# Step sizes of a selective scan: one Softplus on ScalarE out of PSUM, in place of Abs, Relu, Exp, Ln and three GpSimd passes

## The chip, the core and the metric

One NeuronCore of a Trainium2 chip runs the whole kernel. The metric is the device time of one execution in microseconds (us), the median of several runs. Engine names in the profile: PE is TensorE, PEld its weight loads, DVE is VectorE, ACT is ScalarE, POOL is GpSimd, SP is SyncE, which here only issues DMAs. L795 means line 795 of the kernel before.

## What is computed

The reference has two layers on an image of 256 x 256 tokens with 128 channels: layer 0 is a normalised attention along rows (triangle attention), layer 1 a two-dimensional selective scan (the heart of a Mamba block). The change lies in layer 1, in its first line:

```python
def selective_scan(xs, dts, As, Bs, Cs, Ds, dt_bias):
    delta = jax.nn.softplus(dts + dt_bias[None, :, :, None])
    ...
    def step(h, inp):
        d_t, x_t, B_t, C_t = inp
        dA = jnp.exp(d_t[..., None] * As)
        h = dA * h + (d_t * x_t)[..., None] * B_t[:, :, None, :]
        y = jnp.einsum('bkdn,bkn->bkd', h, C_t)
        return (h, y)
```

There are four scan directions (K = 4), 65,536 tokens in each, 256 channels and 16 states per channel; everything is float32. `delta` is the step size: softplus(v) = ln(1 + exp(v)) of a projection v plus a bias for each channel.

## The kernel before, in words

Layer 0 and the convolution in front of the scan take the first 5.5 ms of the 32.2 ms. The scan takes the rest, and the change is in it.

**Steps, groups, turns.** The scan goes through the four directions one after another, in four passes of 128 steps; `steps` (L692) lists them. A step is 512 tokens of one direction. It has 8 groups of 32 channels (`g` from 0 to 7); a group's 32 channels by 4 states fill the 128 partitions, and the 16 states are four such sets. So a group has four turns (the loop `for n, i in enumerate((NB, *range(NB)))` in the last block of the kernel), and in each turn ACT makes one factor `dA` (exp(delta A), L1122) and DVE makes one `tensor_tensor_scan` over 512 tokens (L1148). In turn 0 ACT writes the factor `dAl` to SBUF (2 buffers) and the scan's other input, `bl`, comes from PE out of PSUM. In turns 1 to 3 the factor `dA` goes to PSUM (3 buffers) and the other input has been written by a DVE multiplication, `times_B` (L875, 128 x 1536), which DVE does once per group after turn 1. After a group's last scan POOL copies the last column (`hst`, L1167) and multiplies the group's states with C (L1168); PE sums these products (`sums`, L890) later.

**Who sets the order.** The scan is written under a manual schedule: each engine executes its instructions in the order in which the Python code issues them. The preparation of coming steps is therefore written as generators, and in each turn the main loop takes one piece of `prepare(q + 2)` (`piece(preparing)`), one of `turn`, one of each `finish` or `store`, and a given number of pieces of `products`. A `yield` is the end of a piece. All of this is issued in the turn after that turn's `dA` on ACT and before its scan on DVE.

**What `prepare(q)` does (L721 to L804).** It starts in turn 1 of group 5, two steps ahead of its use. PE turns the tokens (`tps`), ACT copies them (`xs`), PE projects them (`pb`), ACT copies that (`bc`, L747), and a DMA sends its B and C rows to DRAM (`bc_d`). PE then makes `pv`, the projected step size, for the two halves of the channels (L758, two PSUM banks out of a pool of two, tag `mm`). From there on, in the kernel before:

- first group of the next step, turns 1 and 2: for each half ACT computes `e` = |v| (Abs, L765) and `delta` = max(v, 0) (Relu, L766) from PSUM;
- turn 3: PE turns B (`tpb`, L770, in the bank pool that `pv` used), ACT computes `e` = exp(-e) (L773), SP issues the DMAs of `B_r` and `C_r` (L779);
- second group: ACT computes `lg` = 1 + e (L785), `du` = lg - 1 (L788) and copies `B_t` (L790); POOL computes e - du (L792), a correction for the rounding of 1 + e;
- third group: turn 0, ACT computes ln(lg) (L795), for which ACT loads another function table, and loads the table of Exp again for the next `dA` (L1122); turns 1 and 2, POOL adds twice (L797, L799) to get `delta`, and SP sends it to DRAM (`de_d`, L801); turn 3, POOL multiplies `du` = delta * xs (L803).

`spread_delta` (L851) brings `de_d` back into `dr`, spread over partitions, for the factors: the first half in group 5 of the step before its use, the second half at the start of group 1 of the step itself. `du` goes to PE for `spread_du` (L861) and `turn` (L806). In the fourth pass `finish` (L947) follows each step: normalisation, gate and output projection, with ACT operations `yn` (L989), `gz` (L1008), `xo` (L1032) and POOL operations of its own, spread over the following step and a half.

Of the kernel before, what the change touches and what calls it, by code (L numbers as in the profile page):

```python
# [8 lines left out]
F32 = mybir.dt.float32  # L9
BF16 = mybir.dt.bfloat16  # L10
AF = mybir.ActivationFunctionType
ALU = mybir.AluOpType
# [4 lines left out]
P = 128  # L17
# [6 lines left out]
DI = 256  # L24
NS = 16
R = 8
K = 4
T = 512
# [38 lines left out]
def attention_and_scan_kernel(  # L67
# [27 lines left out]
    nc = tc.nc  # L95
# [26 lines left out]
    with tc.tile_pool(name="gx", bufs=3) as gx, tc.tile_pool(  # L122
        name="gps", bufs=1, space=PSUM
# [41 lines left out]
    with tc.tile_pool(name="ln", bufs=3) as ln, tc.tile_pool(  # L165
        name="lnps", bufs=3, space=PSUM
# [100 lines left out]
    with tc.tile_pool(name="abias", bufs=1) as ab:  # L267

        bias = ab.tile([P, 2, H, S], F32, name="bias")
# [24 lines left out]
        with tc.tile_pool(name="ablk", bufs=2) as blk, tc.tile_pool(  # L294
            name="arow", bufs=2
        ) as row, tc.tile_pool(name="aps", bufs=2, space=PSUM) as aps:
            for b in range(S // RB):
# [18 lines left out]
                for q in range(BT // 512):  # L316
# [23 lines left out]
                    for rr in range(2):  # L340
# [5 lines left out]
                        for h in range(H):  # L346
# [14 lines left out]
                            for t in range(2):  # L361
# [4 lines left out]
                                    bias=mx[:, h, t : t + 1],  # L366
# [10 lines left out]
                        for h in range(H):  # L377
                            hp = (h % 2) * C
                            tp = aps.tile([P, 2, S], F32, name="atp")
# [57 lines left out]
    with tc.tile_pool(name="cw", bufs=1) as cw, tc.tile_pool(name="cs", bufs=2) as cs:  # L437
# [23 lines left out]
        with tc.tile_pool(name="g2", bufs=1) as g2, tc.tile_pool(  # L461
            name="g2ps", bufs=1, space=PSUM
        ) as g2ps:
            m2, r2 = group_norm_finish(nc, g2, g2ps, stats2, S // RB, ones, neg_half)
            for col, src in ((m_col, m2), (r_col, r2)):
                tp = g2ps.tile([P, P], F32, name="g2t", tag="g2t")
# [171 lines left out]
    sw = ctx.enter_context(tc.tile_pool(name="sw", bufs=1))  # L638
# [4 lines left out]
    dtb_s = sw.tile([P, K, 2], F32, name="dtb_s")  # L643
# [31 lines left out]
    for q in range(4):  # L675
# [1 line left out]
            spread[:, q],  # L677
            ident[:, 32 * q : 32 * q + 32].unsqueeze(1).to_broadcast([P, 4, 32]),
        )
    neg_one = sw.tile([P, 1], F32, name="neg_one")  # L680
    nc.vector.memset(neg_one, -1.0)
    hst = sw.tile([P, NG, NI], F32, name="hst")

    io = ctx.enter_context(tc.tile_pool(name="io", bufs=2))
    wk = ctx.enter_context(tc.tile_pool(name="wk", bufs=2))
    sd = ctx.enter_context(tc.tile_pool(name="sd", bufs=2, space=DRAM))
# [29 lines left out]
    def until(now, then):  # L716

        for _ in range(then - now):
            yield

    def prepare(q):  # L721

        k, a = steps[q]
        xt = loaded.pop(q)
        xs = io.tile([P, 2, T], F32, name="xs", bufs=3)
        tps = []
        for h in range(2):
            tp = sps.tile([P, T], F32, name="tps", tag="mm")
            for j in range(4):
                nc.tensor.transpose(  # L730
                    tp[:, j * P : (j + 1) * P], xt[:, j, h * P : (h + 1) * P], ident
                )
            tps.append(tp)
            yield
        yield from until(2, 5)
        for h, tp in enumerate(tps):
            nc.scalar.copy(xs[:, h, ::-1] if k >= 2 else xs[:, h, :], tp)
            yield
        pb = sps.tile([R + 2 * NS, T], F32, name="pb", tag="mm")
        for h in range(2):  # L740
            nc.tensor.matmul(  # L741
                pb, xw_in[:, k, h, :], xs[:, h, :], start=(h == 0), stop=(h == 1)
            )
        yield
        yield
        bc = io.tile([R + 2 * NS, T], F32, name="bc", bufs=1)
        nc.scalar.copy(bc, pb)  # L747
        bc_d = sd.tile([2 * NS, T], F32, name="bc_d")
        nc.sync.dma_start(bc_d, bc[R:, :])
        yield  # L750


        e = io.tile([P, 2, T], F32, name="e", bufs=1)
        delta = io.tile([P, 2, T], F32, name="delta", bufs=1)
        pvs = []
        for h in range(2):
            pv = sps.tile([P, T], F32, name="pv", tag="mm")
            nc.tensor.matmul(  # L758
                pv, dtw_s[:, k, h * P : (h + 1) * P], bc[:R, :], start=True, stop=True
            )  # L760
            pvs.append(pv)
        yield
        yield
        for h, pv in enumerate(pvs):
            nc.scalar.activation(e[:, h, :], pv, AF.Abs, bias=dtb_s[:, k, h : h + 1])  # L765
            nc.scalar.activation(delta[:, h, :], pv, AF.Relu, bias=dtb_s[:, k, h : h + 1])  # L766
            yield
        tp = sps.tile([P, 4, R + 2 * NS], F32, name="tpb", tag="mm")
        for b in range(4):
            nc.tensor.transpose(  # L770
                tp[:, b, :], bc[:, b * P : (b + 1) * P], ident[: R + 2 * NS, : R + 2 * NS]
            )
        nc.scalar.activation(e, e, AF.Exp, scale=-1.0)  # L773
        B_r = io.tile([P, NB, T], F32, name="B_r")
        C_r = io.tile([P, NI, T], F32, name="C_r")
        for m, t, ni in ((0, B_r, NB), (1, C_r, NI)):
            for j in range(4):
                n = m * NS + NI * j
                nc.sync.dma_start(  # L779
                    t[32 * j : 32 * j + 32],  # L780
                    bc_d[n : n + ni, :].unsqueeze(0).to_broadcast([32, ni, T]),
                )
        yield
        lg = io.tile([P, 2, T], F32, name="lg", bufs=1)
        nc.scalar.activation(lg, e, AF.Identity, bias=1.0)  # L785
        yield
        du = io.tile([P, 2, T], F32, name="du")
        nc.scalar.activation(du, lg, AF.Identity, bias=neg_one)  # L788
        B_t = io.tile([P, 4, R + 2 * NS], F32, name="B_t")
        nc.scalar.copy(B_t, tp)  # L790
        yield
        nc.gpsimd.tensor_tensor(e, e, du, ALU.subtract)  # L792
        yield
        yield
        nc.scalar.activation(lg, lg, AF.Ln)  # L795
        yield
        nc.gpsimd.tensor_tensor(lg, lg, e, ALU.add)  # L797
        yield
        nc.gpsimd.tensor_tensor(delta, delta, lg, ALU.add)  # L799
        de_d = sd.tile([DI, T], F32, name="de_d")  # L800
        nc.sync.dma_start(de_d.rearrange("(h p) t -> p h t", p=P), delta)  # L801
        yield
        nc.gpsimd.tensor_tensor(du, delta, xs, ALU.mult)  # L803
        prepared[q] = xs, de_d, du, B_r, C_r, B_t  # L804

    def turn(q):  # L806
# [272 lines left out]
    ctx.enter_context(tc.manual_schedule())  # L1079
    load(0)  # L1080
    preparing.append(prepare(0))
    drain(preparing)
    load(1)
# [5 lines left out]
    bxs[0, 0] = times_B(0, spread_du(0, 0))  # L1089
    urs[0, 1] = spread_du(0, 1)  # L1090
    preparing.append(prepare(1))
    for _ in range(2 * NI + 3):
        piece(preparing)
# [9 lines left out]
    for s, (q, g) in enumerate(all_steps):  # L1103
        k, a = steps[q]
# [12 lines left out]
        for n, i in enumerate((NB, *range(NB))):  # L1117
# [23 lines left out]
            if g == 5 and n == 1 and q + 2 < NQ:  # L1141
                preparing.append(prepare(q + 2))
# [91 lines left out]
```

## Time and profile before

| | |
|---|---|
| median of 3 runs | 32186.01 us (32183.83 to 32190.26) |
| the profiled execution, span from first to last instruction | 32185.1 us |
| mean granted TensorE clock | 0.853 |
| busy in the span | PE 23853.4, DVE 29575.2, ACT 25201.0, POOL 25710.4 us |
| first `times_B` of the four passes | at 5576, 12139, 18690 and 25241 us |
| end of the last scan | at 32134 us |

The profile is of one execution. Times in the timeline are us from the start of the span; a group's line gives its count, its busy time and the mean duration of one instruction, and then how long the engine was idle before such instructions, and which engine's work ended most of that idle time. Consecutive instructions of one engine overlap a little, so the distance from start to start (the pitch) is shorter than the duration. The span and the median differ by 1 us, so a sum made against the span can be read against the median.

### The profile page before, as it was taken

Reading aid. Unit: us, or ns where it says so; the run is one execution under the profiler, and the core shown is the slowest. Engines: PE = TensorE matmul, PEld = TensorE weight load, DVE = VectorE, ACT = ScalarE, POOL = GpSimd, SP = SyncE. Lnnn points to the kernel's source line nnn. Section 1 sums busy time; section 2 is a strip of 40 time slices with the busy share of each in tenths; the row PEclk is TensorE's granted clock in tenths of the full one; section 3 lists DMA queues with packets and bytes.
Section 4 is the critical chain, followed back from the end, with each engine's and each line's share of the span. In section 5 each row is a group of like instructions: output and inputs, shape, how many; then the busy total and the mean of one; then the engine's idle time right before and its main releaser. Section 6 shows DMA issues by size and latency. Waiting matters only on the chain.

```text
span 32185.1 us, 380702 instructions
## 1 busy us (share of the span) xinstructions
PE 23853.4 (74%) x122902; PEld 10868.3 (34%) x122902; DVE 29575.2 (92%) x29023; ACT 25201.0 (78%) x50438; POOL 25710.4 (80%) x11291
## 2 busy tenths in 40 slices
PE   6999988666676667777777777777777777777777
PEld 3555544222222222222222232223222333333333
DVE  7666633999999999999999999999999999999999
ACT  5555522888888888888888888888888888888888
POOL 4222200999999999999999999999999999999998
PEclk9999999888888888888888888888888888888888
DMA  4001033444444444444444444444444555555554
GB/s 143 30 28 29 27 105 121 110 109 108 111 109 108 110 110 118 119 121 120 119 120 122 119 119 121 121 119 119 122 119 118 123 124 124 123 123 123 124 123 113
DMA packets 2100469, 3518.55 MB, mean 109 GB/s; under 512 B 201112, under 2 KB 1187096, under 8 KB 2022560
## 3 DMA queue, kind: packets, MB, share of 16 engines
q1 hardware_dynamic: 2093296, 3476.09, 43.3%
q8 instruction: 967, 15.84, 0.2%
q10 hardware_dynamic: 5168, 18.12, 0.1%
q14 instruction: 1038, 8.50, 0.1%
HBM read 2754.18 MB, written 739.25 MB: 109 GB/s over the span
## 4 chain that ended last, share of the span: by engine, by line
PE 32%; ACT 24%; DVE 22%; issue 12%; POOL 9%; DMA 2%; SPq 0%; ACTq 0%; POOLq 0%; DVEq 0%
DVE bx L1148 11%; PE yp L890 8%; DVE bx L875 7%; ACT dA L1122 6%; PE ur L864 6%; POOL bx L1168 5%; PE pb L741 3%; ACT bt L834 2%; PE pc L563 2%; ACT dAl L1122 2%; PE av L393 2%; PE tpy L913 2%; POOL at L370 2%; ACT e L765 2%; ACT L795 2%
## 5 line engine op out<-in xcount | busy, mean ns | idle before, releaser
L1168 POOL TENSOR_TENSOR bx<-bx,C_r 128x2048 f32<-128x2048 f32 x4096 | 18604.4, 4542 | 334.3 <-POOL hst L1167 5.8
L1148 DVE TENSOR_TENSOR_SCAN bx<-dA,hst,bx 128x512 f32<-128x512 f32 x12192 | 15074.4, 1264 | 217.2 <-ACT dA L1122 215.3
L1122 ACT ACTIVATE dA<-dr,A_s 128x512 f32<-128x512 f32 x12288 | 8329.3, 683 | 2247.5 <-DVE bx L1148 2199.6
L864 PE MATMUL ur<-du,spread 128*128 128x512 f32 x8192 | 5710.1, 787 | 4498.5 <-DVE bx L875 4378.8
L875 DVE TENSOR_TENSOR bx<-B_r,ur 128x1536 f32<-128x1536 f32 x4096 | 7075.5, 1727 | 40.1 <-DMA dr<-de_d 40.1
L834 ACT ACTIVATE bt<-duT,B_t 128x128 f32<-128x128 f32 x16384 | 5572.5, 392 | 698.7 <-PE bl L846 698.7
L1148 DVE TENSOR_TENSOR_SCAN bx<-dAl,hst,bl 128x512 f32<-128x512 f32 x4064 | 5096.6, 1254 | 24.2 <-PE bl L846 24.1
L890 PE MATMUL yp<-bx,gather 128*32 128x512 f32 x32768 | 5052.5, 771 | 7.5 <-POOL bx L1168 6.4
L846 PE MATMUL bl<-ident,bt 128*128 128x128 f32 x16384 | 2714.8, 289 | 2441.0 <-DVE bx L1148 2439.0
L846 PEld LDWEIGHTS bl<-ident,bt 128*128 128x128 f32 x16384 | 1791.0, 143 | 4323.4 <-DVE bx L1148 3240.7
L864 PEld LDWEIGHTS ur<-du,spread 128*128 128x128 f32 x8192 | 1451.2, 223 | 5027.9 <-DVE bx L875 5023.9
L370 POOL TENSOR_TENSOR at<-at,sm 128x2048 f32<-128x2048 f32 x256 | 922.2, 3603 | 2719.7 <-DVE sm L369 2550.6
L1122 ACT ACTIVATE dAl<-dr,A_s 128x512 f32<-128x512 f32 x4096 | 2919.2, 713 | 0.0
L890 PEld LDWEIGHTS yp<-bx,gather 128*32 128x32 f32 x32768 | 1165.1, 139 | 4348.3 <-issue 3834.9
L1167 POOL COPY hst<-bx 128x4 f32<-128x4 f32 x4096 | 771.4, 188 | 1615.5 <-DVE bx L1148 1588.6
L362 ACT ACTIVATE at<-at,mx 128x256 f32<-128x256 f32 x2048 | 1016.1, 498 | 472.5 <-DVE mx L358 468.1
L792 POOL TENSOR_TENSOR e<-e,du 128x1024 f32<-128x1024 f32 x512 | 1202.8, 2349 | 138.3 <-DMA C_r<-bc_d 138.3
L799 POOL TENSOR_TENSOR delta<-delta,lg 128x1024 f32<-128x1024 f32 x512 | 1209.9, 2363 | 40.1
L803 POOL TENSOR_TENSOR du<-delta,xs 128x1024 f32<-128x1024 f32 x512 | 1205.4, 2354 | 40.2
L758 PE MATMUL pv<-bc,dtw_s 8*128 8x512 f32 x2048 | 1019.6, 616 | 256.5 <-ACT bc L747 256.5
L797 POOL TENSOR_TENSOR lg<-lg,e 128x1024 f32<-128x1024 f32 x512 | 1205.0, 2354 | 0.2 <-ACT lg L795 0.2
L391 DVE COPY aT<-atp 128x512 f32<-128x512 f32 x512 | 353.6, 691 | 774.8 <-PE atp L382 771.0
(173 smaller groups left out, 31933.7 us busy)
## 6 DMA issues: line engine op xcount, KB each, us to landing
dr<-de_d SPq DMA_DIRECT2D x4096, 256.0 KB
C_r<-bc_d SPq DMA_DIRECT2D x2048, 256.0 KB
B_r<-bc_d SPq DMA_DIRECT2D x2048, 192.0 KB
de_d<-delta SPq DMA_DIRECT2D x512, 512.0 KB
xtok<-xc_d SPq DMA_DIRECT2D x256, 512.0 KB
xtok<-xc_d SPq DMA_DIRECT2D x512, 256.0 KB
yl<-y_d SPq DMA_DIRECT2D x512, 256.0 KB
y_d<-yt SPq DMA_DIRECT2D x512, 256.0 KB
```

The source lines that it names most:

```text
L370: nc.gpsimd.tensor_tensor(at, at, sm.unsqueeze(3).to_broadcast([P, H, 2, S]), ALU.mult,)
L797: nc.gpsimd.tensor_tensor(lg, lg, e, ALU.add)
L799: nc.gpsimd.tensor_tensor(delta, delta, lg, ALU.add)
L803: nc.gpsimd.tensor_tensor(du, delta, xs, ALU.mult)
L834: nc.scalar.mul(bt[:, b, :, j, :], duT[:, b, h * P : (h + 1) * P].rearrange("t (g c) -> t g c", c=32), B_t[:, b, n : n + 1],)
L846: nc.tensor.transpose(bl[:, b * P : (b + 1) * P], bt[:, b, g % 4].rearrange("t j c -> t (j c)"), ident)
L864: nc.tensor.matmul(ur, spread[:, g % 4].rearrange("p j c -> p (j c)"), prepared[q][2][:, g // 4, :], start=True, stop=True,)
L875: nc.vector.tensor_tensor(bx[:, :NB, :], prepared[q][3], ur.unsqueeze(1).to_broadcast([P, NB, T]), ALU.mult,)
L890: nc.tensor.matmul(yp[32 * g : 32 * g + 32, :], gather, hc[:, i, :], start=(i == 0 and steps[q][0] != ORDER[0]), stop=True, skip_group_che ...
L1122: nc.scalar.activation(dA, dr, AF.Exp, scale=A_s[:, k, g // 4, g % 4, i : i + 1])
L1148: nc.vector.tensor_tensor_scan(hs[:, i, :], dA, hs[:, i, :] if i < NB else bls.pop((q, g)), 0.0 if a == 0 else hst[:, g, i : i + 1], ALU.mult,
L1168: nc.gpsimd.tensor_tensor(hs, hs, prepared[q][4], ALU.mult)
```

## The change

The softplus becomes one ACT instruction for each half, straight from `pv` in PSUM with the bias as operand. The buffers `e`, `lg` and the constant `neg_one` go. The DMA of `delta`, the multiplication `du`, the PE transposes of B, the copy `B_t` and the DMAs of `B_r` and `C_r` stay, in other places:

```diff
-    neg_one = sw.tile([P, 1], F32, name="neg_one")
-    nc.vector.memset(neg_one, -1.0)
...
-        e = io.tile([P, 2, T], F32, name="e", bufs=1)
         delta = io.tile([P, 2, T], F32, name="delta", bufs=1)
...
         for h, pv in enumerate(pvs):
-            nc.scalar.activation(e[:, h, :], pv, AF.Abs, bias=dtb_s[:, k, h : h + 1])
-            nc.scalar.activation(delta[:, h, :], pv, AF.Relu, bias=dtb_s[:, k, h : h + 1])
-            yield
+            nc.scalar.activation(
+                delta[:, h, :], pv, AF.Softplus, bias=dtb_s[:, k, h : h + 1]
+            )
+        de_d = sd.tile([DI, T], F32, name="de_d")
+        nc.sync.dma_start(de_d.rearrange("(h p) t -> p h t", p=P), delta)
+        yield
         tp = sps.tile([P, 4, R + 2 * NS], F32, name="tpb", tag="mm")
         for b in range(4):
             nc.tensor.transpose(
                 tp[:, b, :], bc[:, b * P : (b + 1) * P], ident[: R + 2 * NS, : R + 2 * NS]
             )
-        nc.scalar.activation(e, e, AF.Exp, scale=-1.0)
+        yield
+        du = io.tile([P, 2, T], F32, name="du")
+        nc.gpsimd.tensor_tensor(du, delta, xs, ALU.mult)
+        B_t = io.tile([P, 4, R + 2 * NS], F32, name="B_t")
+        nc.scalar.copy(B_t, tp)
+        yield
         B_r = io.tile([P, NB, T], F32, name="B_r")
         C_r = io.tile([P, NI, T], F32, name="C_r")
...
-        yield
-        lg = io.tile([P, 2, T], F32, name="lg", bufs=1)
-        nc.scalar.activation(lg, e, AF.Identity, bias=1.0)
-        yield
-        du = io.tile([P, 2, T], F32, name="du")
-        nc.scalar.activation(du, lg, AF.Identity, bias=neg_one)
-        B_t = io.tile([P, 4, R + 2 * NS], F32, name="B_t")
-        nc.scalar.copy(B_t, tp)
-        yield
-        nc.gpsimd.tensor_tensor(e, e, du, ALU.subtract)
-        yield
-        yield
-        nc.scalar.activation(lg, lg, AF.Ln)
-        yield
-        nc.gpsimd.tensor_tensor(lg, lg, e, ALU.add)
-        yield
-        nc.gpsimd.tensor_tensor(delta, delta, lg, ALU.add)
-        de_d = sd.tile([DI, T], F32, name="de_d")
-        nc.sync.dma_start(de_d.rearrange("(h p) t -> p h t", p=P), delta)
-        yield
-        nc.gpsimd.tensor_tensor(du, delta, xs, ALU.mult)
         prepared[q] = xs, de_d, du, B_r, C_r, B_t
```

In the order of instructions that ACT gets, a table load stands before the two Softplus and another before the next `dA`; the program has as many table loads as before, but for one in the very first step. They stand in turn 1 of the first group of a step instead of turn 0 of the third. The DMA of `de_d` stands in turn 1 of the first group (it was turn 2 of the third), the PE transposes `tpb` in turn 2 (was 3), `du` and `B_t` in turn 3 of the first group (were turn 3 of the third and turn 1 of the second), the DMAs of `B_r` and `C_r` in turn 0 of the second group (were turn 3 of the first). On SP the second half of `dr` now goes ahead of them.

## The prediction

> **What bounds the kernel now.** I read the page first, for the busy shares and their course over time:
>
> ```profile
> PE 23853.4 (74%) x122902; PEld 10868.3 (34%) x122902; DVE 29575.2 (92%) x29023; ACT 25201.0 (78%) x50438; POOL 25710.4 (80%) x11291
> ...
> DVE  7666633999999999999999999999999999999999
> ACT  5555522888888888888888888888888888888888
> POOL 4222200999999999999999999999999999999998
> ```
>
> DVE and POOL both show 9 in the scan (from slice 8 on), so shares do not say which of them sets the pace. The busy time in the four passes of the scan does (columns: stretch, its length, then PE, PEld, DVE, ACT, POOL):
>
> ```profile
> 5576.00:12139.00 6563.00, 4574.31 (x19427) 1793.22 (x19426) 6522.89 (x5118) 5554.67 (x10766) 5992.81 (x2558) 0.83 0.45 109
> 12139.00:18690.00 6551.00, 4663.03 (x20471) 1923.14 (x20470) 6524.59 (x5121) 5556.56 (x10753) 6000.74 (x2561) 0.83 0.49 120
> 18690.00:25241.00 6551.00, 4670.14 (x20481) 1930.03 (x20482) 6524.16 (x5121) 5557.31 (x10756) 6000.26 (x2561) 0.83 0.49 120
> 25241.00:32134.00 6893.00, 5056.47 (x23700) 2427.97 (x23698) 6730.30 (x6139) 5981.81 (x11599) 6495.85 (x3191) 0.82 0.51 123
> ```
>
> DVE is idle for 26 us of the second pass, and for 163 us of the fourth. It is the bound, and the change touches no DVE instruction. POOL's own waits are mostly for DVE (L1167: 1615.5 us idle, 1588.6 of it for the scan). So the large removals (three POOL passes of 2.35 us, 7.1 us per step) do not count by themselves; only DVE's waits do. Those of the fourth pass:
>
> ```profile
> DVE bx L1148 <- ACT dA L1122: 148.6, 125, 1.9
> ```
>
> 125 waits in 128 steps: one per step, at one place. The other passes have 27.4, 21.1 and 20.2 us of the same kind. The timeline of a step in the second pass shows the place, the Ln of the third group:
>
> ```profile
> 15016.30 0.73 ACT L1122 ACTIVATE dAl<-dr,A_s 128x512 f32<-128x512 f32 x1
> 15017.05 1.28 ACT L795 ACT_TABLE_LOAD   x1
> 15018.34 1.06 ACT L795 ACTIVATE lg<-lg 128x1024 f32<-128x1024 f32 x1
> ...
> 15019.42 1.28 ACT L1122 ACT_TABLE_LOAD   x1
> 15019.98 1.25 DVE L1148 TENSOR_TENSOR_SCAN bx<-dAl,hst,bl 128x512 f32<-128x512 f32 x1
> ...
> 15020.71 1.91 ACT L1122 ACTIVATE dA<-dr,A_s 128x512 f32<-128x512 f32 x3
> ...
> 15021.44 1.28 DVE L1148 TENSOR_TENSOR_SCAN bx<-dA,hst,bx 128x512 f32<-128x512 f32 x1 [0.20 <-ACT dA L1122]
> ```
>
> From 15017.05 to 15020.71 ACT makes no factor; the scan in turn 1 starts when the factor after it is there.
>
> **What the waits cost.** A group without waits takes 6.36 us (`times_B` starts at 15041.72 and next at 15048.08), eight take 50.88. The second pass took 6551/128 = 51.18 per step, so 0.30 us is lost: some 0.2 is shown as idle, the rest is overlap of instructions that a wait breaks. In three passes that is 384 x 0.30 = 115 us. In the fourth pass `finish` adds DVE work: there `times_B` at 28015.69 is followed by a scan at 28018.93, 3.24 us instead of 1.64, so a step without waits takes 50.88 + 1.57 = 52.45 (the scan behind it is 0.03 shorter). It took 6893/128 = 53.85: 1.40 lost, 179 us in the pass.
>
> **What is removed.** Per step ACT loses two Abs and two Relu from PSUM (0.57 us of pitch each), Exp, 1 + e and Ln (1.06 each) and `du` (1.15), and gets two Softplus. The Ln block leaves the third group, and with it the waits on L1122. The two table switches do not go; they move.
>
> **What is added, and its room.** In the first group, turn 1, ACT now does: load, Softplus, Softplus, load, and only then the next `dA`. A load is 1.283 us wherever it occurs (L795, L1122, and for other functions L313, L362). Softplus is in no row. Nearest is Abs of L765: the same PSUM tile, shape and bias operand, 0.673 us, pitch 0.57. The plain copy out of PSUM (L737, 0.577) bounds it from below, as an instruction of this shape; `gz` with two pointer operands (0.768) is the dearest single pass. I take Abs. As Softplus has to do what Abs, Relu, Exp and Ln did together, two passes (1.24 us) are the upper end, kept for a rival. The block then is 1.28 + 0.57 + 0.67 + 1.28, the next `dA` 0.68, and about 0.1 for gaps and the signal to DVE: 4.58 us. The rows of the turn before:
>
> ```profile
> 15005.45 0.67 ACT L1122 ACTIVATE dA<-dr,A_s 128x512 f32<-128x512 f32 x1
> 15006.07 0.67 ACT L765 ACTIVATE e<-pv,dtb_s 128x512 f32<-128x512 f32 x1
> ...
> 15011.25 2.45 DVE L1148 TENSOR_TENSOR_SCAN bx<-dA,hst,bx 128x512 f32<-128x512 f32 x2
> ```
>
> `dA` ends at 15006.12 and the next scan out of PSUM is due at 15011.25: room 5.13, margin 0.55. Abs started at 15006.07 without idle, so `pv` is ready. The block is hidden by two scans and `times_B`; without that cover it would cost all of 3.8 us. In these passes I cost it at nothing.
>
> In the fourth pass two `yn` (0.5 us of pitch each) stand ahead, and `bc` waits for PE:
>
> ```profile
> 28039.04 0.67 ACT L1122 ACTIVATE dA<-dr,A_s 128x512 f32<-128x512 f32 x1
> ...
> 28044.35 2.44 DVE L1148 TENSOR_TENSOR_SCAN bx<-dA,hst,bx 128x512 f32<-128x512 f32 x2
> ```
>
> Room 4.64 here. Over neighbouring steps it runs through 5.52, 4.64, 4.21, 3.99, 4.23 and again, as `yp` on PE takes between 4.1 and 5.8 us under the clock it is granted. Against 4.58 that misses by 0.37, 0.59 and 0.35 in three steps of five: 0.26 us on average, 0.31 with broken overlap, 40 us in the pass. The scan after it is due 1.2 us later and its factor takes 0.6, so it does not wait again.
>
> Waits for `bl` from PE (14 us in the fourth pass, 10 in the second and third) may shrink, since ACT is ahead in group 3, where `bl` depends on its products; I take it that these 24 us stay.
>
> **What is moved.** On POOL `du` comes before the first group's `hst`: POOL is free of the last product at 15012.2, ends `du` at 14.6 and starts `hst` 0.8 us late (it was 15013.76, after 1.5 idle); with the passes of the next groups gone it has caught up a group later. On SP the DMA of `de_d` now waits for Softplus (until about 15008.7) ahead of `dr`, `B_r`, `C_r`. That half of `dr` is needed three groups later, `B_r` and `C_r` a step later, and `C_r` waited for POOL until 15012.24 anyway. On PE `tpb` needs the bank of the first Softplus half, at 15008.0 instead of 15007.36; behind it `bl` waits for a scan until 15008.56. All hidden.
>
> **The start.** The very first step has nothing beside it: `pv` is done at 5555.4, `de_d` issued at 5569.9, first `times_B` at 5576.23. Now two Softplus end at 5556.7 (the load fits in ACT's wait of 1.2 us for `pv`); then SP issues `B_r` and `C_r`, 3.5 us, so `dr` goes out about 5561 instead of 5572.96: 12 us earlier, and the rest follows from it. If `B_r` lands late, 8.
>
> **Sum.** (115 - 10) + (179 - 40 - 14) + 12 = 242; 32185 - 242 = **31,943 us**, -0.75%.
>
> In the timeline above a load begins 0.02 us after the instruction before it and the next begins 0.01 us after the load: no drain on either side. The Trainium skill ("ScalarE: Activation LUTs", section "What ACT_TABLE_LOAD costs") speaks against this place: it gives a switch of sets 1283 ns and a drain of about 1380 ns, 2.66 us in all. By the page the block would be an estimated 7.3 us, 2.2 over the room in every step of three passes, and the change slower by some 900 us. The sum goes by the rows.
>
> **Rivals.**
>
> 1. *The wait moves with the block, and is dearer: slower.* The place is turn 1 of the first group; the mechanism is a Softplus longer than Abs. With x us more per step, three passes lose 384 (x - 0.47) once the margin is gone, the fourth 128 x. Together they reach 242 at x = 0.82, or 0.41 us per Softplus. Two passes each (1.24 us, x = 1.14) give 257 + 146 = 403: 31,943 + 403 = **32,346**. For it: no row has the function. Against: the instruction order shows one instruction per half, and Abs (0.673), Exp (0.683) and Sigmoid (0.688, L313) take alike for 512 elements. 10%.
> 2. *No change*: the same with x between 0.70 and 0.97, or unseen gaps of that size around the loads, 32,120 to 32,260. 6%.
> 3. *The fourth pass keeps its loss*, as the block meets `yn` and a late `bc` in every step: 32,185 - 105 - 12 = **32,068**. For it: the margin is negative in three steps of five already. 7%.
> 4. *POOL is the bound after all*, and gives back 3 x 2.35 x 512 = 3.6 ms. Against: DVE's idle time above. 1%.
>
> **How the numbers follow.** The forecast has 76%. Within it: all waits gone 31,880; the fourth pass missing by 0.7 in every step, Softplus at 0.77 and a smaller gain at the start, 32,000. The range reaches to rival 3: 31,880 to 32,070 leaves out 17%. A measurement tells 0.2%, 64 us, from no change. Faster: 76 + 7 + 1 = 84%; same 6%; slower 10%.
>
> **What would show it.** Softplus at 0.67 us, its loads at 1.283 and no drain; no DVE wait in the third group; in the first three passes none in the first group either and 50.9 us per step; in the fourth waits of 0.3 to 0.6 us at turn 2 of the first group, about 52.9 per step; `times_B` first at about 5564. Softplus over 1.1 us, or DVE waits in every first group, would make me wrong.

## The result, and the profile after

The kernel with the change takes 32,224.97 us (median of 20 runs, 32,219.26 to 32,233.03); the kernel before, measured beside it, 32,180.05 (20 runs, 32,169.77 to 32,190.26). The ratio is 1.0014 with a 95% interval of 1.0007 to 1.0020. The forecast was 31,943, range 31,880 to 32,070: wrong in sign, by 282 us. The profiled execution has a span of 32,226.3 us.

The page of the kernel after, its busy shares and slices:

```profile
PE 24360.0 (76%) x122902; PEld 11354.2 (35%) x122902; DVE 29552.8 (92%) x29022; ACT 22794.7 (71%) x47365; POOL 22239.6 (69%) x9755
...
DVE  7666633999999999999999999999999999999999
ACT  5555522777777777777777777777777777777777
POOL 4222200777777777777777777777777888888887
```

The work is gone as intended: POOL is busy 3,471 us less (25,710.4 before), ACT 2,406 us less, and their slices fall from 9 and 8 to 7 (POOL's to 8 in the fourth pass). DVE has the same work, the same 92%, and sets the end as before. The four passes of the scan (stretch, length, then PE, PEld, DVE, ACT, POOL, clock, DMA share and GB/s):

```profile
5563.00:12087.00 6524.00, 4726.30 (x19428) 1956.28 (x19428) 6508.44 (x5118) 4958.60 (x10000) 5123.30 (x2174) 0.80 0.47 110
12087.00:18639.00 6552.00, 4807.33 (x20469) 2044.64 (x20468) 6516.92 (x5121) 4954.04 (x9984) 5130.54 (x2177) 0.81 0.49 120
18639.00:25193.00 6554.00, 4807.66 (x20480) 2046.90 (x20480) 6516.55 (x5121) 4955.46 (x9986) 5130.12 (x2177) 0.81 0.49 120
25193.00:32175.00 6982.00, 5130.91 (x23700) 2521.45 (x23700) 6737.40 (x6138) 5381.22 (x10839) 5641.07 (x2810) 0.81 0.51 121
```

Here the loss has its place. The first pass is 39 us shorter than before, the second 1 us longer, the third 3 longer, the fourth 89 longer. The first pass differs from the others in one thing that matters: it has no earlier pass whose `y_d` it adds to, so `load_sum` (L884) loads no `yl`. What DVE waits for in the fourth pass of the kernel after (total, times, longest):

```profile
DVE bx L1132 <- PE bl L830: 210.7, 120, 3.7
DVE bx L1132 <- ACT dA L1106: 28.3, 69, 0.6
```

The 148.6 us of waiting for the factor behind the Ln are gone, and DVE now waits 210.7 us for `bl`. Nearly all of it, 209.7 us, is at one place in the step, the first scan of the fifth group (group 4 counted from 0). PE, in turn, waits for this, first in the kernel after from 12,100 to 32,000 us:

```profile
PE ysum L897 <- DMA yl<-y_d: 176.0, 92, 3.2
PE tpy L897 <- DMA yl<-y_d: 98.8, 109, 1.9
```

and in the kernel before from 12,200 to 31,900 us:

```profile
PE tpy L913 <- DMA yl<-y_d: 14.7, 34, 1.4
PE ysum L913 <- DMA yl<-y_d: 4.4, 13, 0.8
```

275 us instead of 19. One step of the fourth pass shows how the wait reaches DVE (timeline of the kernel after; the number in brackets is the idle time before, and what ended it):

```profile
27724.06 2.05 PE L897 MATMUL ysum<-yl,ident 128*128 128x512 f32 x2 [1.21 <-DMA yl<-y_d]
...
27725.90 1.92 PE L902 MATMUL ysum<-ident,yo 128*128 128x128 f32 x8
...
27727.60 1.91 PE L897 MATMUL ysum<-yl,ident 128*128 128x512 f32 x2
...
27729.31 1.37 PE L902 MATMUL ysum<-ident,yo 128*128 128x128 f32 x8
...
27730.52 0.60 PE L830 MATMUL bl<-ident,bt 128*128 128x128 f32 x4
...
27731.22 1.28 DVE L1132 TENSOR_TENSOR_SCAN bx<-dAl,hst,bl 128x512 f32<-128x512 f32 x1 [1.78 <-PE bl L830]
```

PE takes its instructions in order. It stands 1.21 us until `yl` has landed, does the two halves of the sum (6.6 us at the clock of this stretch), and only then comes to `bl`, which has nothing to do with `yl` but stands behind it. DVE has had nothing to scan for 1.78 us.

Why `yl` is late is on SP's queue. A step of the second pass after (T, the start of its first scan, is 15,776.98):

```profile
15777.27 0.38 SPq L766 DMA_DIRECT2D de_d<-delta  x1
15777.69 2.36 SPq L840 DMA_DIRECT2D dr<-de_d  x4
15780.17 2.65 SPq L784 DMA_DIRECT2D B_r<-bc_d  x4
15783.37 3.83 SPq L784 DMA_DIRECT2D C_r<-bc_d  x4
15787.84 1.18 SPq L891 DMA_DIRECT2D yl<-y_d  x2
```

and the step at the same place before (T = 15,826.47):

```profile
15824.60 1.71 SPq L779 DMA_DIRECT2D B_r<-bc_d  x4
15831.45 1.70 SPq L779 DMA_DIRECT2D C_r<-bc_d  x4
15833.56 1.74 SPq L856 DMA_DIRECT2D dr<-de_d  x4
15835.40 1.19 SPq L907 DMA_DIRECT2D yl<-y_d  x2
...
15849.64 0.36 SPq L801 DMA_DIRECT2D de_d<-delta  x1
```

Before, `B_r` went out 1.9 us ahead of T, `yl` at T + 8.9, and `de_d` (0.5 MB) long after it, at T + 23. After, SP issues nothing until `delta` is there at T + 0.3, then `de_d` and the twelve transfers of `dr`, `B_r` and `C_r` follow each other, and `yl` goes out last, at T + 10.9 (medians of the second pass: T + 10.0 after, T + 8.7 before). The four of `C_r` take 3.83 us instead of 1.70, though a single issue is no longer than before (median 0.30 us, 0.42 before). What is longer are SP's waits between them: the program's DMAs take eight semaphores in turn, and so a DMA of this step goes out only when the one eight places before it has landed. `C_r` waits so for the four of `dr`, and `yl` for those of `B_r`. SP's waits in the kernel after, from 12,100 to 18,600 us:

```profile
SPq L784 <- DMA dr<-de_d: 331.9, 404, 1.8
SPq L891 <- DMA B_r<-bc_d: 123.7, 249, 1.5
```

and in the kernel before, from 12,139 to 18,690 us, where `C_r` is what stands eight ahead of `yl`:

```profile
SPq L907 <- DMA C_r<-bc_d: 39.2, 85, 1.3
```

The 16 DMA engines in the same step of the kernel after (the last two columns are DMA share and GB/s):

```profile
15773.00:15777.00 4.00, 3.16 (x14) 1.22 (x12) 4.00 (x5) 3.97 (x6) 2.56 (x1) 1.00 0.07 18
15777.00:15781.00 4.00, 0.81 (x7) 0.45 (x5) 4.00 (x5) 3.97 (x7) 3.79 (x2) 0.86 0.73 220
...
15785.00:15789.00 4.00, 4.00 (x33) 1.21 (x25) 4.00 (x4) 1.45 (x3) 4.00 (x1) 0.78 1.08 237
15789.00:15793.00 4.00, 1.62 (x7) 0.55 (x6) 4.00 (x4) 3.52 (x8) 3.10 (x3) 1.00 0.97 201
15793.00:15797.00 4.00, 2.50 (x3) 0.96 (x4) 4.00 (x4) 2.47 (x7) 2.35 (x3) 0.57 0.90 248
```

The DMA engines stand almost idle (0.07) just before T and are full from there to T + 20, about when PE wants `yl`.

The chain that ended last says the same in one line of the page; this is the kernel after:

```profile
DVE bx L1132 23%; DVE bx L859 12%; PE yp L874 9%; PE ur L848 6%; DMA yl<-y_d 5%; DMA B_r<-bc_d 3%; PE pc L563 2%; PE av L393 2%; POOL at L370 2%; PE atp L382 2%; PE bl L830 2%; PE pb L739 1%; PE tpy L897 1%; PE ysum L897 1%; DVE at L357 1%
```

`yl` and `B_r` are on it; in the kernel before no DMA is in this line.

### The profile page after: what moved, and what is told of

It is laid out like the page before. It is cut to its first block, busy times and chain, and to the rows that moved or that the text cites. A ratio compares the mean times of both kernels' runs of the same rounds, so it can differ in the third digit from the quotient of the medians.

```text
span 32226.3 us, 374544 instructions
## 1 busy us (share of the span) xinstructions
PE 24360.0 (76%) x122902; PEld 11354.2 (35%) x122902; DVE 29552.8 (92%) x29022; ACT 22794.7 (71%) x47365; POOL 22239.6 (69%) x9755
## 4 chain that ended last, share of the span: by engine, by line
DVE 39%; PE 35%; issue 11%; DMA 8%; ACT 5%; POOL 2%; SPq 1%; DVEq 0%; POOLq 0%; ACTq 0%
DVE bx L1132 23%; DVE bx L859 12%; PE yp L874 9%; PE ur L848 6%; DMA yl<-y_d 5%; DMA B_r<-bc_d 3%; PE pc L563 2%; PE av L393 2%; POOL at L370 2%; PE atp L382 2%; PE bl L830 2%; PE pb L739 1%; PE tpy L897 1%; PE ysum L897 1%; DVE at L357 1%
## 5 line engine op out<-in xcount | busy, mean ns | idle before, releaser
L1132 DVE TENSOR_TENSOR_SCAN bx<-dA,hst,bx 128x512 f32<-128x512 f32 x12192 | 15043.4, 1260 | 28.3 <-ACT dA L1106 28.3
L830 PE MATMUL bl<-ident,bt 128*128 128x128 f32 x16384 | 2833.8, 299 | 1856.6 <-DVE bx L1132 1852.7
L830 PEld LDWEIGHTS bl<-ident,bt 128*128 128x128 f32 x16384 | 1914.1, 150 | 3713.4 <-DVE bx L1132 2719.8
L739 PE MATMUL pb<-xs,xw_in 128*40 128x512 f32 x2048 | 981.0, 601 | 0.0
L728 PEld LDWEIGHTS tps<-ident,xtok 128*128 128x128 f32 x4096 | 806.3, 211 | 432.0 <-issue 432.0
L389 ACT COPY aT<-atp 128x512 f32<-128x512 f32 x512 | 300.1, 586 | 921.8 <-PE atp L382 589.6
```

Source lines behind the costliest of these rows:

```text
L739: nc.tensor.matmul(pb, xw_in[:, k, h, :], xs[:, h, :], start=(h == 0), stop=(h == 1))
L830: nc.tensor.transpose(bl[:, b * P : (b + 1) * P], bt[:, b, g % 4].rearrange("t j c -> t (j c)"), ident)
L1132: nc.vector.tensor_tensor_scan(hs[:, i, :], dA, hs[:, i, :] if i < NB else bls.pop((q, g)), 0.0 if a == 0 else hst[:, g, i : i + 1], ALU.mult,
```

## The experiments

**Theory A:** the load of `yl` lands too late behind the burst on SP's queue; PE waits for it in order, and `bl` with it. Two parts of it can be told apart. **A1:** SP itself stands still at `de_d`, which waits for the Softplus, and holds back `dr`, `B_r`, `C_r` and `yl`. **A2:** the 0.5 MB of `de_d` are now moved ahead of `yl`. **Theory B:** with the Ln gone, PE's own chain up to `bl` is the next bound, and `yl` only shows where.

e1 to e4 ran on one chip, where the kernel before takes 32,179.61 us, e5 to e7 on another, where it takes 32,190.97. Ratios are to the kernel before on the same chip.

**e1_old_places: both DMA groups back in their old places, the new Softplus kept.**

```diff
-        de_d = sd.tile([DI, T], F32, name="de_d")
-        nc.sync.dma_start(de_d.rearrange("(h p) t -> p h t", p=P), delta)
         yield
...
-        du = io.tile([P, 2, T], F32, name="du")
-        nc.gpsimd.tensor_tensor(du, delta, xs, ALU.mult)
-        B_t = io.tile([P, 4, R + 2 * NS], F32, name="B_t")
-        nc.scalar.copy(B_t, tp)
-        yield
         B_r = io.tile([P, NB, T], F32, name="B_r")
...
+        du = io.tile([P, 2, T], F32, name="du")
+        nc.gpsimd.tensor_tensor(du, delta, xs, ALU.mult)
+        B_t = io.tile([P, 4, R + 2 * NS], F32, name="B_t")
+        nc.scalar.copy(B_t, tp)
+        yield
+        yield from until(15, 21)
+        de_d = sd.tile([DI, T], F32, name="de_d")
+        nc.sync.dma_start(de_d.rearrange("(h p) t -> p h t", p=P), delta)
         prepared[q] = xs, de_d, du, B_r, C_r, B_t
```

> Softplus on ACT as in the changed kernel, but SP gets its DMAs where the kernel before had them: B_r and C_r in turn 3 of the first group, de_d in turn 2 of the third. Theory A (the DMA of yl lands too late, because dr, B_r, C_r and de_d now go out in one burst ahead of it, and PE holds bl behind yl): yl is issued as before, about 9 to 10 us after the step's first scan, the DVE waits for bl shrink to under 0.1 us per step in the second and third pass and under 0.4 in the fourth, 31,930 to 31,990 us. Theory B (with the wait at Ln gone, PE's own work in the fourth group is the bound, wherever yl comes): the waits stay at 0.3 and 1.7 us per step, 32,170 to 32,240 us.

Measured: 31,956.11 us, 0.9931 of before (0.9916 to 0.9945). What is left of PE's and DVE's waits from 12,100 us on:

```profile
PE tpy L898 <- DMA yl<-y_d: 23.3, 35, 1.6
```

```profile
DVE bx L1133 <- PE bl L831: 42.2, 90, 1.8
...
DVE bx L1133 <- ACT dA L1107: 26.3, 62, 0.4
```

The new Softplus with the old places gives what the forecast said, within 13 us. So the loss is in the moved DMAs, not in the function. A little of it is left: in passes 2 and 3 a step takes 0.11 us more than in e2, below. `yl` goes out as before there (T + 8.7, medians of the second pass), but with the wait at the Ln gone PE is through with the work ahead of it at T + 18.7, not T + 19.0. So some of the margin of `yl` was that wait; whether `de_d`, which now goes out at T + 13, takes a part in these 0.11 us is not told apart.

**e2_de_d_late: only the DMA of `de_d` goes back** (the first and the last part of the diff above; `B_r` and `C_r` stay behind `dr`).

> The changed kernel with only the DMA of de_d back in turn 2 of the third group; B_r and C_r stay behind dr. Theory A: yl goes out behind 0.5 MB less and no later than about 8 us after the first scan, 31,930 to 31,990 us. If only the place of B_r and C_r counts, and not the bytes of de_d nor its wait: 32,150 to 32,230 us. Theory B: 32,170 to 32,240 us.

Measured: 31,929.04 us, 0.9923 (0.9908 to 0.9937). PE has no wait for `yl` at all, and DVE's waits for `bl` from 12,100 us on are

```profile
DVE bx L1133 <- PE bl L831: 18.4, 65, 0.6
```

Moving this one DMA gives back 296 us, the whole loss, and 27 us more than e1, in which `B_r` and `C_r` go ahead of `dr` again. SP issues `yl` at T + 8.0 in a step of the second pass (median of the pass T + 6.8). What came back is the place in SP's order, not the time: `delta` has long been there, and SP issues `de_d` at T + 9.0 (median of the second pass) behind `yl`, where before it waited for POOL until T + 23.

**e3_BC_early: only `B_r` and `C_r` go back ahead of `dr`**, and `de_d` stays ahead of both.

> The changed kernel with only the DMAs of B_r and C_r back in turn 3 of the first group, ahead of dr; de_d stays early, ahead of them. Theory A: yl is issued about 1 us earlier than in the changed kernel but the same bytes are ahead of it, so part of the waits stay: 31,960 to 32,120 us. If only the order on SP counts: 31,930 to 31,990 us. Theory B: 32,170 to 32,240 us.

Measured: 32,225.78 us, 1.0015 (1.0005 to 1.0024): no gain at all, where A had expected some; by its number alone this run lies in the range of theory B. DVE in the stretch from 12,100 us on:

```profile
DVE bx L1132 <- PE bl L830: 303.4, 250, 2.4
```

The place of `B_r` in the program helps nothing while `de_d` is in front of it: SP issues `B_r` 0.8 us after T, and as many transfers as in the kernel after stand between `de_d` and `yl`. A's number for this run was wrong: the order among the transfers behind `de_d` changes nothing when `de_d` is what holds them all. `yl` does go out earlier, at T + 8.8 (median of the second pass), almost where it was in the kernel before, and PE still waits 256 us for it. So an early issue alone does not bring it in time.

**e4_yl_first: `de_d` stays early; `yl` is loaded two groups sooner**, at the start of the step, into a second buffer.

```diff
-        yl = io.tile([P, 4, DI], F32, name="yl", bufs=1)
+        yl = io.tile([P, 4, DI], F32, name="yl", bufs=2)
...
-        yn = io.tile([P, 4, DI], F32, name="yn", tag="yl", bufs=1)
+        yn = io.tile([P, 4, DI], F32, name="yn", tag="yl", bufs=2)
...
-        if g == 2 and q and steps[q - 1][0] != ORDER[0]:
+        if g == 0 and q and steps[q - 1][0] != ORDER[0]:
             summed[q - 1] = load_sum(q - 1)
```

> The changed kernel with the load of yl in group 0 instead of group 2, so ahead of de_d, dr, B_r and C_r on SP, and two buffers for it. Theory A: PE never waits for yl, DVE waits for bl under 0.1 us per step in the second and third pass, under 0.4 in the fourth, 31,920 to 31,980 us. Theory B: PE's chain is as long as before, waits of 0.3 and over 1 us per step stay, 32,100 to 32,230 us.

Measured: 31,923.66 us, 0.9920 (0.9906 to 0.9935), which e2, e5 and e7 match within their intervals. PE never waits for `yl`, and from 12,100 us on DVE waits

```profile
DVE bx L1132 <- ACT dA L1106: 26.1, 62, 0.4
DVE bx L1132 <- PE bl L830: 18.0, 64, 0.3
```

PE's work is the same as in the kernel after, and so are `de_d`, `dr`, `B_r` and `C_r`; only `yl` no longer stands behind them. (The second buffer also spares `yl` a wait for `yn`, which shares its buffer in the fourth pass; in the kernel after SP waits 12 us in all for that, and in e2 466 us without any wait of PE for `yl`, so this is not the loss.) Theory B falls: PE's own chain costs 18 us in all. These are also the two waits that the forecast had left.

**e5_de_d_on_ACT: the same 0.5 MB, 1.4 us later in the step, but ACT issues them**, so that nothing on SP waits for the Softplus.

```diff
-        de_d = sd.tile([DI, T], F32, name="de_d")
-        nc.sync.dma_start(de_d.rearrange("(h p) t -> p h t", p=P), delta)
         yield
         tp = sps.tile([P, 4, R + 2 * NS], F32, name="tpb", tag="mm")
...
+        de_d = sd.tile([DI, T], F32, name="de_d")
+        nc.scalar.dma_start(de_d.rearrange("(h p) t -> p h t", p=P), delta)
         yield
```

> The changed kernel with the DMA of de_d issued by ACT, after the next factor (turn 2 of the first group), so that SP does not wait for Softplus there; its 0.5 MB still move ahead of C_r and yl. Theory A1 (the harm is that SP stands still until Softplus ends, with dr and B_r behind it, so that the burst starts some 4 us later): SP sends dr and B_r about 3 us ahead of the step's first scan, PE does not wait for yl, 31,925 to 31,990 us. Theory A2 (the harm is the 0.5 MB that go ahead of yl): the waits stay mostly, 32,100 to 32,230 us.

Measured: 31,931.26 us, 0.9919 (0.9905 to 0.9934). SP in a step of the second pass (T = 15,752.75):

```profile
15750.65 1.73 SPq L840 DMA_DIRECT2D dr<-de_d  x4
15752.48 1.77 SPq L784 DMA_DIRECT2D B_r<-bc_d  x4
15757.74 6.71 SPq L784 DMA_DIRECT2D C_r<-bc_d  x4
15764.55 0.89 SPq L891 DMA_DIRECT2D yl<-y_d  x2
```

`dr` goes out 2.1 us ahead of T, where in the kernel after it is 0.7 behind it. `yl` is issued no earlier than in the kernel after (here T + 11.8 against T + 10.9, medians of the second pass T + 10.0 in both), and still no sum on PE waits for it: the DMA engines began their work earlier and have less in front of it. From T + 8 to T + 12 their share is 0.47 here and 1.08 in the step of the kernel after. So what counts is not when `yl` is issued but when the engines are through with what was given to them before; e3, with an early issue and the waits, says the same. With SP free, the bytes cost nothing: A1 is needed for the loss. Since the bytes here come through another queue and `dr` and `B_r` are ahead of them, this run does not tell what 0.5 MB ahead of `dr` on SP's own queue cost without the wait.

The Trainium skill ("DMA: Bandwidth & Descriptors", section "Issuing engines are not separate DMA queues") says that issuing from several engines saves only the sequencer's time to initiate a DMA, usually small beside the transfer. The issue took 0.38 us on SP and 0.37 on ACT, so that saving is small here too; what the run gained, some 305 us (0.9919 against 1.0014), came from the wait in front of the issue, which the sentence does not cover.

**e6_SP_waits_only: SP waits for the Softplus as in the kernel after, but for a transfer of one row** (2 KB, an added store that nobody reads); the 0.5 MB go late, as in e2.

```diff
-        de_d = sd.tile([DI, T], F32, name="de_d")
-        nc.sync.dma_start(de_d.rearrange("(h p) t -> p h t", p=P), delta)
+        row = sd.tile([1, T], F32, name="row")
+        nc.sync.dma_start(row, delta[0:1, 1, :])
...
+        yield from until(15, 21)
+        de_d = sd.tile([DI, T], F32, name="de_d")
+        nc.sync.dma_start(de_d.rearrange("(h p) t -> p h t", p=P), delta)
```

> SP waits for Softplus at the same place, but only for one row of delta (2 KB, to a scratch buffer); the DMA of de_d itself goes out late, in turn 2 of the third group. Theory A1: the burst starts as late as in the changed kernel, most of the waits stay, 32,120 to 32,230 us. Theory A2: 0.5 MB less ahead of yl is about 2.3 us at 220 GB/s, the waits go, 31,930 to 32,000 us. If each does a part: both this run and the one with ACT's queue lie between.

Measured: 32,025.16 us, 0.9948 (0.9933 to 0.9962). It lies between the two expectations. From 12,100 us on:

```profile
PE ysum L900 <- DMA yl<-y_d: 86.2, 84, 2.6
PE tpy L900 <- DMA yl<-y_d: 19.2, 33, 1.3
```

```profile
DVE bx L1135 <- PE bl L833: 98.1, 122, 1.5
```

Against e5, on the same chip, SP's standing still costs 32,025 - 31,931 = 94 us; against e2, which differs only in the added row, it is some 80 us by the ratios. With the 0.5 MB in front of the rest, in the kernel after, it is some 305. The two are no separate terms of a sum, since the bytes beside a free SP (e5) cost nothing that can be told from e2. As I read it, each delays `yl`: the standing puts `dr` and all behind it off by about 3 us (T + 0.7 against T - 2.1 in e5), the bytes by some 2.4 us (0.5 MB at the 220 GB/s of the window above), and PE feels only what goes beyond the time at which it wants `yl`.

**e7_both: e2 and e4 together.**

> The two versions that took the waits away, put together: de_d late and yl in group 0 with two buffers. If yl was the only thing late on that path there is nothing more to take: 31,905 to 31,930 us, the same as the better of the two. If the DMA burst also delays something else that DVE waits for, under 31,900 us.

Measured: 31,925.81 us, 0.9917 (0.9901 to 0.9934). As near to e4 as can be told: either of the two is enough, and the second adds nothing that can be told.

Length of a step in each pass, from first scan to first scan, mean of 126 steps, in us (forecast: as predicted, not measured):

| kernel | pass 1 (no `yl`) | pass 2 | pass 3 | pass 4 |
|---|---|---|---|---|
| before | 51.21 | 51.19 | 51.18 | 53.88 |
| forecast | 50.9 | 50.9 | 50.9 | 52.9 |
| after | 50.88 | 51.21 | 51.21 | 54.59 |
| e1 | 50.89 | 51.00 | 51.00 | 52.90 |
| e2 | 50.89 | 50.89 | 50.90 | 52.90 |
| e3 | 50.89 | 51.19 | 51.21 | 54.60 |
| e4 | 50.89 | 50.90 | 50.89 | 52.90 |
| e5 | 50.89 | 50.89 | 50.89 | 52.90 |
| e6 | 50.89 | 50.98 | 51.00 | 53.51 |
| e7 | 50.89 | 50.90 | 50.91 | 52.90 |

## Why the prediction was wrong

**What was right.** DVE is the bound, and its waits decide. Those behind the Ln went, and the passes without a new wait run at the forecast length. Softplus costs what Abs does. ACT's rows of the kernel after from 5,500 us on:

```profile
L762 ACT ACT_TABLE_LOAD x512 | 656.9, 1283 | 9.0
L1106 ACT ACT_TABLE_LOAD x512 | 656.9, 1283 | 9.0
L762 ACT ACTIVATE delta<-pv,dtb_s 128x512 f32<-128x512 f32 x1024 | 648.4, 684 | 6.2
```

0.684 us beside the 0.673 of Abs, loads of 1.283. The block in a step of the second pass, which begins right behind the last `dA`:

```profile
15774.68 1.28 ACT L762 ACT_TABLE_LOAD   x1
15775.97 1.27 ACT L762 ACTIVATE delta<-pv,dtb_s 128x512 f32<-128x512 f32 x2
...
15777.26 1.28 ACT L1106 ACT_TABLE_LOAD   x1
...
15778.55 1.30 ACT L1106 ACTIVATE dA<-dr,A_s 128x512 f32<-128x512 f32 x2
```

From the load to the next `dA` it takes 3.87 us (forecast 3.8), and DVE has no wait for a factor in the second and third pass. No run here shows a drain around a load. By the Trainium skill ("ScalarE: Activation LUTs", section "What ACT_TABLE_LOAD costs") the block would be an estimated 2.8 us longer, two drains of about 1.38; the measurement decides. In the fourth pass the trace of the kernel after gives 0.22 us per step (28.3 us in 128 steps) at the forecast place, turn 2 of the first group (forecast 0.26, 0.31 with broken overlap). The first `times_B` starts at 5,563.7 (forecast 5,564). So rivals 1, 2 and 3 all failed: 1 and 2 because Softplus is no dearer, 3 because the fourth pass did lose its Ln wait. Rival 4 failed as well: POOL's 3,471 us bought nothing by themselves. That the time came near to "no change" is not rival 2, whose mechanism is a longer Softplus.

**The step that failed** is "What is moved", and in it the sentence on SP with its "All hidden". It looked at `dr`, `B_r` and `C_r` behind the waiting `de_d` and found a use far enough away for each; it stopped there. The next transfer on the queue, `yl` of `load_sum`, issued at the start of the third group, was not named, and the 0.5 MB of `de_d` that now go ahead of it were not counted. The runs put in its place: PE waits for `yl` for 275 us instead of 19, and `bl` with it; that is 0.32 us per step in passes 2 and 3 (51.21 against 50.89), 1.69 in the fourth (54.59 against 52.90), or 256 x 0.32 + 128 x 1.69 = 298 us against e4, where the two spans differ by 304. The span is 283 us over the forecast.

**The 24 us of waits for `bl`** that "stay" were the warning. I took them for a constant. In the profile before 13 of them stand before the first scan of the fifth group, the place behind `yl`. PE waited for `yl` 47 times there, 19 us in all: `yl` landed just about when it was wanted, in some steps later. With `yl` in time (e4) there is none at that place; the 18 us that are left stand elsewhere, 17 of them at the second group in the fourth pass. A step that had asked what ends PE's own waits ahead of `bl`, instead of keeping DVE's 24 us, would have found `yl` without margin, and then SP's queue in front of it.

**The rest of "What is moved"** held: in the timeline of a second-pass step POOL's `du` puts `hst` about 0.7 us late (forecast 0.8), and no wait of DVE follows. On PE, `tpb` now waits for the Softplus (471 us in all from 12,100 us on in the kernel after), and e4 has the same wait (461.7) at 50.89 us per step, so it costs nothing.

**The clock** is no cause in passes 1 to 3. It fell from 0.83 to 0.80 and 0.81 there, which could look like the reason; but the first pass of the kernel after was the shorter one at 0.80, and e4 was granted 0.80 in all three and takes 50.9 us per step. In the fourth pass e4 had 0.84 and the kernel after 0.81; whether the lower clock made the waits behind `yl` longer there is not told apart.

## What to carry to other kernels

An instruction that is made to wait on a queue delays everything behind it, so follow the queue past the transfers next to it, up to the first one whose user already waits for it now and then; in the profile here that was a row with a small total and many times (19 us in 47 waits), and it meant that the margin was gone. When a move removes work from engines that are not the bound, its gain comes only from the bound's waits, and its price from the order of transfers: here 256 us of gain were in the new function (e4), and 296 were lost by the place of one DMA (e2). Send a result out where its wait stands in front of nothing urgent, or load the urgent thing first.

## What the runs showed of the hardware

- The step of the kernel before was 51.18 to 51.21 us in three passes, which is close to 15 x 3.413 us. In its trace the granted clock changes in stretches of multiples of 3.413 us: of 3,184 stretches 627 last 3.413, 1,399 last 6.827, 205 last 10.240 and 817 last 13.653 us. With the wait at the Ln gone, steps of 50.89 are no such multiple; in the fourth pass of the kernel after the median step is 54.60, and 16 x 3.413 is 54.61. Whether the clock's stretches hold a step that waits for PE at such a length, and so set the size of a loss, was not tried.
- Less work on ACT and POOL went with a lower TensorE clock in the first three passes (0.83 before; 0.80 and 0.81 after), while PE did the same matmuls; PE's busy time rose by 507 us, in e4 by 386, and there it cost nothing.
- SP's rows of several issues hold waits: the four issues of `C_r` took 1.70 us before, 3.83 in the kernel after and 6.71 in e5. In the two long rows SP waits between the issues until an earlier DMA has landed: the pieces of `dr` in the kernel after, and `de_d` in e5, between the first issue of `C_r` at 15,757.74 and the second at 15,763.22.
